# GRU, attention and AUGRU on one core: the last GRU step, the last softmax blocks and the way into the AUGRU rearranged

## The chip, the cores and the metric

The kernel runs on one core of one Trainium2 chip. Its engines work in parallel, each through its own queue in order: TensorE (PE, with its weight loads as PEld), VectorE (DVE), ScalarE (ACT), GpSimd (POOL) and SyncE (SP, which issues DMAs). The metric is the device time of one execution in microseconds (us).

## The reference

For 1024 samples and 100 steps of 128 features, the reference computes, all in float32:

```python
hist_sum = (hist * mask).sum(1) / length
keys = GRU(hist)                                  # all 100 states, 128 wide
score = relu-MLP([keys, q, keys - q, q * keys])   # 512 -> 80 -> 40 -> 1, q the item
attn = softmax(where(mask == 1, score, -inf), over the 100 steps)
pooled = einsum('bt,btd->bd', attn, keys)         # [1024, 128]
att_seq = pooled.T[:100]                          # row t weighs step t of the AUGRU
# AUGRU over keys, from a state of zeros
r = sigmoid(Wr [h, x]); u = att_seq[t] * sigmoid(Wu [h, x])
h = (1 - u) * h + u * tanh(Wh [h * r, x])
state = AUGRU state at step length - 1
scores = sigmoid-MLP([user, item, hist_sum, item * hist_sum, state])
```

The AUGRU therefore needs the attention over all 100 steps before its first step.

## The kernel before

The 1024 samples are two halves of 512; features lie on the partitions, samples along the free axis. `gru_phase` runs the 100 GRU steps, and `augru_phase` the 100 AUGRU steps after it. In both, the program order of each engine is written out by hand (`manual_schedule`), with the two halves staggered.

**GRU steps.** For each step `s` and half, `Half.gru` (L482 to L527) has PE compute the gates into PSUM banks, ACT the sigmoids and the tanh, and DVE the sums; the state `hn` is the key of that step. One step behind, `transpose` (L529 on) puts the key into blocks of 32 by 32 in a tile `kt` of four steps and stores `kt` to `keys_d` once it is full (L547, 1 MB for each half and four steps). `product` (L559) multiplies the key by the item, `attend` (L646) runs the three small layers of the score MLP packed in the PE, one layer for each of three successive steps, and `take` two calls later adds and applies the relu on DVE and ACT (L680 to L687) and stores a row of scores, by a small DMA, to `s_b` (L692). So the score of step `s` reaches `s_b` at loop step `s + 4`.

**Softmax by blocks.** When the last score of a block in `ENDS` is in, `softmax` queues three stages: `scores(0)` (transposes the scores of half 0), `tops` (those of half 1, the new maxima, the differences, L732 to L746) and `sums` (after `exponents`, the Exp on ACT, L752: products with the mask and the denominators, L755 to L769). `stage()` runs one a step on DVE, after half 0's GRU of the step. `sums` appends a rescaling (if it is not the first block) and the block's keys to each half's `todo`. `pool` (L572 to L583) takes one or two keys a step from it, on POOL, a product and a sum each. `history` (L476, L477) is also POOL's: the masked sum of the inputs, at the loop step of its input. Inputs `x` and masks are loaded two steps ahead by SP.

**After the last step.** From L850 on, what is left is written out: the last two attention layers, the softmax of the last blocks (whose `e` and products then use the PSUM banks named in `banks`), the first layer of the final MLP for what does not depend on the AUGRU (`features`, L613, stored at L623), and the last poolings, half 0's on POOL and half 1's on DVE. The pooled sums are masked (L908) and stored to `pooled_d` by eight DMAs on SP (L911).

**Into the AUGRU.** The AUGRU works on samples sorted by length, so that finished ones drop out. POOL gathers the sorted rows of `pooled_d` (`gather_weights`, L135), then sorted keys. PE transposes the keys of steps 0 and 1 (`load_key`, L987, L988), `first_step` (L935, L937) computes the gates of step 0, `open_gates` (L1001) the input parts of step 1. `sort_weights` (L952 to L967) spreads row 0 of the weights over the partitions by matmuls and forms the first state, transposes all 100 rows to `att_d`, and loads rows 1 and 2 from there, spread over the partitions (L974). `half_step` (L1020 on) is one step of one half: it closes the gates (L1005), weighs `pu` by the loaded row (L1036) and opens the next step. `sort_weights(0)` runs ahead of step 1, `sort_weights(1)` within half 0's step 1.

PSUM has eight banks: `ps` has six and `pa` two in the GRU, `ps3` seven and `pa3` one in the AUGRU, on the same memory in order. The AUGRU's first user of a bank waits for the last user of that bank in the GRU part.

## Time and profile before

| | us |
|---|---|
| median of 13 runs | 2091.33 (2087.88 to 2093.91) |
| the profiled execution, time | 2088.67 |
| the profiled execution, span of the trace | 2086.6 |
| GRU step, from one `r` (L502) to the next | 14.07 |
| last state of half 1 done | 1415.2 |
| last product with the mask (L908) done | 1452.8 |
| first gather of sorted weights | 1458.6 |
| first weights spread by PE (half 0) | 1465.2 |
| first candidate gate of step 1 closed by PE (L1005 on `r`) | 1482.9 |

Times inside the execution count from the start of the span. A line of the timeline gives start, duration, engine, line of the kernel, operation, output and inputs, shapes, and in brackets how long the engine had been idle and what ended that. A line by stretch gives for each engine the busy time and, in brackets, the number of instructions. A line of waits gives who waited for whom: total, times, longest.

### The profile page before, as it was taken

The page shows a single profiled execution, that of the slowest core. Times are in us where ns is not written, and L with a number is a line of the kernel's source. Part 1 is how long each engine was busy: PE and PEld are TensorE (multiplying, and loading weights), DVE is VectorE, ACT ScalarE, POOL GpSimd, SP SyncE. Part 2 cuts the span into 40 slices and gives each one's busy share as a digit, 9 for nine tenths or more (in the row PEclk, how much of TensorE's full clock was granted, in tenths as well). Part 3 has the DMA queues.
Part 4 walks back from the last instruction along what each step waited for, and adds up shares of the span by engine and source line. Part 5 has one row for each costly group of instructions (what it writes and reads, how often), then busy time and mean ns, then how long its engine had stood idle before and what let it go on. Part 6 is the DMA issues. An engine that isn't in the chain of part 4 may idle for free. (4 is left out here: it accounts for less than half of the span.)

```text
span 2086.6 us, 26766 instructions
## 1 busy us (share of the span) xinstructions
PE 2038.6 (98%) x8304; PEld 980.4 (47%) x8304; DVE 1748.8 (84%) x3040; ACT 827.6 (40%) x1511; POOL 1299.0 (62%) x1302
## 2 busy tenths in 40 slices
PE   8999999999999999999999999996799999999997
PEld 3343333333333333333333333333344556679897
DVE  6888999989989888989889888997467777888886
ACT  3334343433434333433343333343244444445454
POOL 0234939579796959595969587696645444444332
PEclk9999999999999999999999999998999999999999
DMA  4643233332234334333433222322533333333331
GB/s 119 114 93 101 88 102 110 95 96 89 88 104 111 112 100 121 110 97 108 132 102 98 86 82 84 102 93 69 154 92 116 94 93 96 99 97 101 84 73 34
DMA packets 254612, 205.60 MB, mean 99 GB/s; under 512 B 75847, under 2 KB 216875, under 8 KB 254459
## 3 DMA queue, kind: packets, MB, share of 16 engines
q1 hardware_dynamic: 242138, 171.36, 29.0%
q0 software_dynamic: 12320, 32.44, 5.5%
q8 instruction: 67, 1.10, 0.2%
q14 instruction: 87, 0.70, 0.1%
HBM read 147.68 MB, written 54.40 MB: 97 GB/s over the span
## 5 line engine op out<-in xcount | busy, mean ns | idle before, releaser
L490 PE MATMUL ps<-x,wih 128*128 128x512 f32 x1200 | 592.0, 603 | 4.0 <-DMA x<-in_hist_x 4.0
L490 PE MATMUL ps<-hn,whh 128*128 128x512 f32 x1188 | 574.6, 592 | 0.0
L490 PEld LDWEIGHTS ps<-x,wih 128*128 128x128 f32 x1200 | 220.9, 191 | 326.8 <-issue 254.0
L490 PEld LDWEIGHTS ps<-hn,whh 128*128 128x128 f32 x1188 | 225.9, 190 | 283.9 <-issue 275.5
L476 POOL TENSOR_TENSOR xm<-x,m 128x512 f32<-128x512 f32 x200 | 247.0, 1235 | 127.3 <-DMA m<-mask_d 127.0
L521 ACT ACTIVATE ps<-ps,bih 128x512 f32<-128x512 f32 x200 | 132.4, 662 | 469.8 <-DVE ps L520 469.8
L502 ACT ACTIVATE r<-ps,brz 128x512 f32<-128x512 f32 x200 | 137.4, 687 | 394.9 <-PE ps L490 393.8
L477 POOL TENSOR_TENSOR hist<-hist,xm 128x512 f32<-128x512 f32 x200 | 265.6, 1328 | 15.7
L583 POOL TENSOR_TENSOR pooled<-pooled,kw 128x512 f32<-128x512 f32 x190 | 253.4, 1334 | 14.9
L582 POOL TENSOR_TENSOR kw<-kt,e 128x512 f32<-128x512 f32 x190 | 217.1, 1143 | 64.1 <-DVE e L755 64.0
L159 POOL DMA_INDIRECT rows<-keys_d,idx_k x208 | 202.2, 972 | 84.7 <-POOL rows L158 53.3
L559 DVE TENSOR_TENSOR kq<-hn,item 128x512 f32<-128x512 f32 x200 | 227.3, 1176 | 0.0
L646 PE MATMUL pm<-hn,wk 128*32 128x512 f32 x1200 | 214.3, 600 | 6.0 <-DVE f L680 3.6
L646 PE MATMUL pm<-kq,wkq 128*32 128x512 f32 x1200 | 211.1, 594 | 0.0
L1013 ACT ACTIVATE c<-ph,bh 128x96 f32<-128x96 f32 (+42 forms) x198 | 96.7, 488 | 262.3 <-PE ph L1005 228.5
L646 PE MATMUL pm<-mv,w 128*32 128x512 f32 (+1 forms) x808 | 197.8, 603 | 1.1 <-ACT mv L685 0.9
L1029 DVE TENSOR_TENSOR pu<-pu,c 128x96 f32<-128x96 f32 (+42 forms) x197 | 88.8, 451 | 104.9 <-ACT c L1013 96.1
L680 DVE TENSOR_TENSOR f<-pm,q 128x512 f32<-128x512 f32 x200 | 128.5, 684 | 56.0 <-PE pm L646 56.0
L158 POOL COPY rows<-rest 128x1 f32<-128x1 f32 x208 | 39.0, 188 | 218.4 <-DVE rest L1039 213.2
L525 DVE TENSOR_TENSOR d<-hn,ps 128x512 f32<-128x512 f32 x198 | 136.1, 687 | 34.9 <-ACT ps L521 32.6
L526 DVE TENSOR_TENSOR d<-ps,d 128x512 f32<-128x512 f32 x200 | 138.4, 692 | 23.7 <-ACT ps L522 6.8
L520 DVE TENSOR_TENSOR ps<-ps,u 128x512 f32<-128x512 f32 x200 | 140.0, 700 | 21.6 <-PE ps L490 0.5
(171 smaller groups left out, 3014.1 us busy)
## 6 DMA issues: line engine op xcount, KB each, us to landing
x<-in_hist_x SPq DMA_DIRECT2D x212, 256.0 KB
keys_d<-kt SPq DMA_DIRECT2D x46, 1024.0 KB
m<-mask_d SPq DMA_DIRECT2D x200, 128.0 KB
keys_d<-kt SPq DMA_DIRECT2D x64, 64.0 KB
rows<-keys_d,idx_k POOLq DMA_INDIRECT x208
s_b<-mv SPq DMA_DIRECT2D x200, 8.0 KB
mask_i<-in_mask SPq DMA_DIRECT2D x8, 200.0 KB
at<-att_d SPq DMA_DIRECT2D x32, 48.0 KB
```

The costliest lines, as they stand in the source:

```text
L159: nc.gpsimd.indirect_dma_start(out=r[:, k, :], out_offset=None, in_=keys_d[q], in_offset=bass.IndirectOffsetOnAxis(ap=idx_k[:, k, i : i + ...
L476: nc.gpsimd.tensor_mul(d, x, m)
L477: nc.gpsimd.tensor_add(acc, acc, d)
L490: nc.tensor.matmul(p, lhsT=w[:, g, :], rhs=v, start=(j == 0), stop=(j == len(parts) - 1),)
L502: nc.scalar.activation(r, pr, AF.Sigmoid, bias=brz[:, 0:1])
L520: nc.vector.tensor_add(pi, pi, u)
L525: nc.vector.tensor_sub(d, h, pi)
L526: nc.vector.tensor_mul(d, pz, d)
L559: nc.vector.tensor_mul(kq, h, item[:, self.cols])
L582: eng.tensor_mul(d, k, w)
L583: eng.tensor_add(acc, acc, d)
L646: nc.tensor.matmul(p[i][s, :], lhsT=w[:, s], rhs=v, start=start, stop=stop)
```

## The change

Eight things change together.

- `ENDS` has blocks that end at 80, 86, 90, 93, 96, 98, 100 where it had 80, 88, 92, 96, 98, 100: one block more, and the block pending at the end of the loop (93 to 95) is of three steps and not of four.
- In step 99 no softmax stage runs. The block that becomes due there runs its first two stages after `attend(T - 1)`, and its Exp and third stage further down.
- From step 84 on, `history` takes the input of the following step (at 84 both), and in step 99 none; POOL also pools one key a half, or two, in step 99, after the products for the final MLP.
- In the written-out end the order of features, stages and poolings changes, the block pending there copies its weights later, and half 1 pools one key (not two) on DVE ahead of the next scores.
- The store of the last four keys moves from the transpose of the last step to after the last scores.
- The banks named in `banks` are assigned in another order.
- The pooled sums of half 1 come first and are stored by SP; those of half 0 are stored by ACT, from `augru_phase`, after the keys of step 0.
- The weights of step 1 are spread by matmuls and copied by ACT, as row 0 is spread by matmuls; only rows from 2 on go through `att_d`, and that store comes later, within step 1. The keys of step 1 go through the one bank of `pa3`.

```diff
-ENDS = (*range(8, 89, 8), 92, 96, 98, T)
+ENDS = (*range(8, 81, 8), 86, 90, 93, 96, 98, T)
...
-                x, m = self.x.pop(t), self.m.pop(t)
+                x, m = self.x[t], self.m.pop(t)
...
-                elif n == G - 1:
-                    row, part = divmod(q - WHOLE, 2)
-                    nc.sync.dma_start(
...
+                elif n == G - 1 and t < T - 1:
+                    self.store(q)
+
+            def store(self, q):
+                row, part = divmod(q - WHOLE, 2)
+                nc.sync.dma_start(
...
-        late, again = 6, 24
+        late, again, early_from = 6, 24, 84
...
-                    stage(2 if last else 1)
+                    stage(0 if last else 1)
...
-            for half in halves:
-                if s >= late:
-                    half.history(s)
-                else:
-                    half.x.pop(s)
+
+            for n_x in range(s + (s > early_from), min(s + (s >= early_from), T - 1) + 1):
+                for half in halves:
+                    if n_x >= late:
+                        half.history(n_x)
             for half in halves:
                 if last:
                     half.cross_features()
-                else:
-                    half.pool(2 if len(half.todo) > 7 or s >= 92 else 1, nc.gpsimd)
+            for half in halves:
+                half.pool(2 if len(half.todo) > 7 or s >= 92 else 1, nc.gpsimd)
...
-        banks.update(e=names[:2], kw=names[2], pt=names[3], f=names[4:])
+        banks.update(e=[b[0], b[1]], kw=b[3], pt=b[2], f=[b[4], b[5]])
...
         attend(T - 1)
-        stage()
-        e, _ = soft["e"]
-        copy = banks["e"][0][:, : NK * (G + 1)].rearrange("p (k n) -> p k n", n=G + 1)
-        nc.vector.tensor_copy(copy, e[:, :, : G + 1])
-        for half in halves:
-            half.todo = [((w[0], copy if w[0] is e else None), n, t) for w, n, t in half.todo]
-        halves[0].pool(T, nc.gpsimd)
+        stage(2)
+        weights = soft["e"][0]
+        exponents()
+        some(0, 1)
+        take(T - 1)
+        some(0, 1)
+        attend(T)
+        some(2)
         for half in halves:
             half.transpose(T - 1)
-        some(features[:1])
-        take(T - 1)
-        some(features[:1])
-        attend(T)
-        some(features[1:2])
-        halves[1].pool(2, nc.vector)
+        stage()
+        n = ENDS[-3] - ENDS[-4] + 1
+        copy = banks["e"][0][:, : NK * n].rearrange("p (k n) -> p k n", n=n)
+        nc.vector.tensor_copy(copy, weights[:, :, :n])
...
+        halves[0].pool(T, nc.gpsimd)
+        halves[1].pool(1, nc.vector)
         stage()
         take(T)
...
         attend(T + 1)
...
         stage()
         take(T + 1)
         exponents()
-        some(features[2:4])
+        some(3, 4)
+        some(5, 6)
+        for half in halves:
+            half.store((T - 1) // G)
         halves[1].pool(T, nc.vector)
-        some(features[4:6])
         stage()
         halves[0].pool(T, nc.gpsimd)
+        some(5, 6)
+        some(7)
         stage(2)
...
-        for half in halves:
+        for half in reversed(halves):
             t = blocked(s_bs[NH * (soft["j"] % 2) + half.i])
             nc.vector.tensor_mul(t, later["used"][:, half.ks, :], pooled[:, half.ks, :])
             to = pooled_d[half.cols, :].rearrange("(k r) (p c) -> p r k c", r=R, c=R)
-            for p in range(P // R):
-                nc.sync.dma_start(out=to[p], in_=t[p * R : (p + 1) * R])
+            later["att", half.i] = [(to[p], t[p * R : (p + 1) * R]) for p in range(P // R)]
+        for to, t in later["att", 1]:
+            nc.sync.dma_start(out=to, in_=t)
...
-        def sort_weights(i, r, gates):
+        def weight_row(t, i, p):
             for g in range(GH):
                 nc.tensor.matmul(
+                    p[:, ts(g, P)],
+                    lhsT=sorted_rows[i][:, g, t : t + 1].to_broadcast([P, P]),
                     rhs=ident,
...
+        def first_state(i, p):
+            weight_row(0, i, p)
+            u, h = gates[i]
+            nc.vector.tensor_mul(p, p, u)
+            nc.vector.tensor_mul(h3[i], p, h)
+
+        def first_weights(i, p):
+            weight_row(1, i, p)
+            at = att[1, i] = wp.tile([P, HB], F32, name="at", bufs=6)
+            nc.scalar.copy(at, p)
+
+        def store_weights(i, p):
             for g in range(GH):
-                nc.tensor.transpose(p[:, ts(g, P)], r[:, g, :], ident)
+                nc.tensor.transpose(p[:, ts(g, P)], sorted_rows[i][:, g, :], ident)
             rows_t = wp.tile([P, HB], F32, name="att_t", bufs=2)
             nc.vector.tensor_copy(rows_t, p)
             nc.sync.dma_start(out=att_d[i], in_=rows_t[:T, :])
-            for t in (1, 2):
-                load_att(t, i)
+            load_att(2, i)
...
-                p = bank("pk3") if t < 2 else pa.tile([P, HB], F32, tag="a", name="pk3")
+                p = pa.tile([P, HB], F32, tag="a", name="pk3")
...
             if t == 1 and i == 0:
-                sort_weights(1, sorted_rows[1], gates[1])
+                store_weights(0, pa.tile([P, HB], F32, tag="a", name="pw"))
+                first_state(1, spare)
+            elif t == 1:
+                first_weights(1, spare)
             nc.vector.tensor_mul(pu, pu, att.pop((t, i))[:, :w])
...
+            if t == 1 and i:
+                store_weights(1, spare)
             if t + 2 < T:
                 load_att(t + 2, i)
...
-        sorted_rows = [gather_weights(i) for i in range(NH)]
         for i in range(NH):
             load_key(0, i)
+        for to, t in later["att", 0]:
+            nc.scalar.dma_start(out=to, in_=t)
+        sorted_rows = [gather_weights(i) for i in range(NH)]
         gates = [first_step(i) for i in range(NH)]
...
-        sort_weights(0, sorted_rows[0], gates[0])
+        spare = bank("spare")
+        first_state(0, pa.tile([P, HB], F32, tag="a", name="first"))
+        first_weights(0, spare)
```

More of the change, by code (lines that the diff above doesn't have):

```diff
@@ L544, in transpose @@
                         )
-                elif n == G - 1:
-                    row, part = divmod(q - WHOLE, 2)
-                    nc.sync.dma_start(
-                        out=keys_d[WHOLE + row].rearrange("(k p) m -> p k m", p=P)[
-                            :, self.ks, ts(part, G * R)
-                        ],
-                        in_=kt.rearrange("p k n c -> p k (n c)"),
-                    )
+                elif n == G - 1 and t < T - 1:
[3 more added lines that the diff above has]
+                nc.sync.dma_start(
+                    out=keys_d[WHOLE + row].rearrange("(k p) m -> p k m", p=P)[
+                        :, self.ks, ts(part, G * R)
+                    ],
+                    in_=self.kt[q].rearrange("p k n c -> p k (n c)"),
+                )
             def product(self, t):
@@ L853, in gru_phase, with some @@
         all_of(rest)
-        names = [ps.tile([P, HB], F32, tag="g", name="last") for _ in range(6)]
-        banks.update(e=names[:2], kw=names[2], pt=names[3], f=names[4:])
+        b = [ps.tile([P, HB], F32, tag="g", name="last") for _ in range(6)]
+        banks.update(e=[b[0], b[1]], kw=b[3], pt=b[2], f=[b[4], b[5]])
         features = [half.features(g) for half in halves for g in range(GH)]
-        def some(these):
+        def some(*these):
             for f in these:
-                next(f)
+                next(features[f])
         take(T - 2)
@@ L867, in gru_phase @@
         attend(T - 1)
-        stage()
-        e, _ = soft["e"]
-        copy = banks["e"][0][:, : NK * (G + 1)].rearrange("p (k n) -> p k n", n=G + 1)
-        nc.vector.tensor_copy(copy, e[:, :, : G + 1])
-        for half in halves:
-            half.todo = [((w[0], copy if w[0] is e else None), n, t) for w, n, t in half.todo]
-        halves[0].pool(T, nc.gpsimd)
+        stage(2)
[6 more added lines that the diff above has]
+        some(2)
         for half in halves:
             half.transpose(T - 1)
-        some(features[:1])
-        take(T - 1)
-        some(features[:1])
-        attend(T)
-        some(features[1:2])
-        halves[1].pool(2, nc.vector)
+        stage()
[3 more added lines that the diff above has]
+        for half in halves:
+            half.todo = [
+                ((w[0], copy if w[0] is weights else None), n, t) for w, n, t in half.todo
+            ]
+        halves[0].pool(T, nc.gpsimd)
+        halves[1].pool(1, nc.vector)
         stage()
         take(T)
-        some(features[1:2])
+        some(2)
         attend(T + 1)
-        some(features[2:4])
+        some(3, 4)
         stage()
@@ L890, in gru_phase @@
         exponents()
-        some(features[2:4])
+        some(3, 4)
+        some(5, 6)
+        for half in halves:
+            half.store((T - 1) // G)
         halves[1].pool(T, nc.vector)
-        some(features[4:6])
         stage()
         halves[0].pool(T, nc.gpsimd)
+        some(5, 6)
+        some(7)
         stage(2)
-        some(features[4:6])
         exponents()
-        some(features[6:])
-        some(features[6:])
+        some(7)
         stage()
@@ L945, in gather_weights @@
             return r
-        def sort_weights(i, r, gates):
-            first = pa.tile([P, HB], F32, tag="a", name="first")
+        def weight_row(t, i, p):
             for g in range(GH):
                 nc.tensor.matmul(
-                    first[:, ts(g, P)],
-                    lhsT=r[:, g, 0:1].to_broadcast([P, P]),
+                    p[:, ts(g, P)],
+                    lhsT=sorted_rows[i][:, g, t : t + 1].to_broadcast([P, P]),
                     rhs=ident,
@@ L958, in sort_weights @@
                 )
-            u, h = gates
-            nc.vector.tensor_mul(first, first, u)
-            nc.vector.tensor_mul(h3[i], first, h)
-            p = pa.tile([P, HB], F32, tag="a", name="pw") if i else bank("pw")
+        def first_state(i, p):
[8 more added lines that the diff above has]
+        def store_weights(i, p):
             for g in range(GH):
-                nc.tensor.transpose(p[:, ts(g, P)], r[:, g, :], ident)
+                nc.tensor.transpose(p[:, ts(g, P)], sorted_rows[i][:, g, :], ident)
             rows_t = wp.tile([P, HB], F32, name="att_t", bufs=2)
```

## The prediction

> **What bounds the kernel now.** I read the page's forty slices first, then the busy time by stretch, then the waits of DVE and PE between 1399 and 1490 us, and last the timelines of that stretch, because the change touches nothing else.
>
> The slices: PE is at nine tenths everywhere but for a dip at slices 28 to 29, and POOL and DVE dip there too.
>
> ```profile
> PE   8999999999999999999999999996799999999997
> DVE  6888999989989888989889888997467777888886
> ```
>
> By stretch (PE, its weight loads, DVE, ACT, POOL; then TensorE clock, DMA share, GB/s): the reader is to see a PE that is full before and after, and holes between.
>
> ```profile
> 1300.00:1400.00 100.00, 100.00 (x397) 38.66 (x396) 91.62 (x136) 41.12 (x64) 77.98 (x64) 1.00 0.33 102
> ...
> 1432.60:1452.80 20.20, 8.23 (x47) 7.64 (x46) 18.66 (x46) 3.40 (x10) 11.32 (x10) 0.81 0.12 43
> 1452.80:1458.60 5.80, 5.80 (x18) 3.02 (x17) 0.00 (x0) 4.02 (x6) 0.00 (x0) 0.77 0.53 90
> ...
> 1470.60:1482.90 12.30, 2.27 (x12) 1.70 (x11) 3.06 (x5) 0.10 (x1) 6.05 (x7) 0.72 0.70 216
> 1482.90:1488.50 5.60, 5.60 (x11) 2.35 (x11) 2.31 (x5) 2.60 (x4) 3.75 (x8) 0.70 0.51 174
> 1500.00:1900.00 400.00, 399.90 (x1318) 241.85 (x1317) 309.71 (x604) 178.92 (x327) 185.44 (x316) 1.00 0.36 100
> ```
>
> So GRU steps and AUGRU steps are PE-bound, and the passage between them (about 1406 to 1486 us) is a chain of waits. Time taken from that chain moves all later work forward one for one; time on DVE or POOL inside the steps is free while PE stays full. The waits in the passage:
>
> ```profile
> DVE first L960 <- PE first L952: 13.6, 1, 13.6
> DVE first L960 <- remote: 7.8, 1, 7.8
> DVE last L732 <- DMA s_b<-mv: 4.1, 1, 4.1
> ...
> PE pk L987 <- DVE pooled L583: 9.7, 1, 9.7
> PE pw L964 <- DVE h L961: 9.1, 1, 9.1
> PE pm L646 <- DVE f L680: 3.6, 1, 3.6
> ```
>
> Four links can be read: a DVE that is late in the last step (PE waits 3.6), scores that land late (4.1), a PE that waits for the end of pooling before it starts the AUGRU (9.7), and the start of the AUGRU itself (13.6, 7.8, 9.1). In DVE's timeline the cause of the 3.6 and the end of pooling stand as
>
> ```profile
> 1406.63 0.72 DVE L732 STREAM_TRANSPOSE pt<-s_b 128x512 f32<-128x512 f32 x1
> ...
> 1409.38 1.38 DVE L746 TENSOR_TENSOR e<-e,top 128x128 f32<-128x128 f32 x1
> 1410.67 0.74 DVE L510 SCALAR_TENSOR_TENSOR u<-ps,bhh,r 128x512 f32<-128x512 f32 x1
> ...
> 1451.48 1.28 DVE L908 TENSOR_TENSOR s_b<-used,pooled 128x512 f32<-128x512 uint8 x2
> ```
>
> **The change part by part.** I follow milestones in the profiled execution.
>
> *Stages out of step 99.* DVE's eight softmax instructions from 1406.63 to 1410.67 leave. Half 1's gate inputs were ready at 1405.65, so its state is done 4.04 us sooner: 1415.2 becomes 1411.2. They are not saved but moved: DVE does them after the products of the last step. PE, which finished the attention of step 98 at 1412.2, finds the bank free at about 1411.9 instead of 1415.9, so its 3.6 us hole closes, and with it most of the half clock behind it (clock 0.59 from 1415.2 to 1422.8). What then limits is the product kq (2.7 us, to 1415.7); attention of step 99 ends near 1417.4, not 1422.8.
>
> *Shorter last blocks.* One block more: per block about 7.8 us of DVE in three steps (0.95, 3.2 and 3.6 by the rows of steps 95 to 97), and two more rescalings on POOL (1.07 each). They fall in steps with a PE of 100.00 in 100; three-step blocks take DVE 39 to 41 us of 42.2, so six such steps in a row (93 to 98) still fit: cost 0. If that cover is gone the excess of DVE, at most a microsecond or two, is paid. The block pending at the end has 3 keys instead of 4: one product and one sum less for each half in the tail, 1.4 us on DVE, 2.3 on POOL.
>
> *History a step ahead.* Four POOL instructions per step (4.9 us) run one step sooner; no DMA moves, since x and mask are loaded two steps ahead. In step 99 POOL drops 4.9 us of history and takes two poolings of 2.4 us. By POOL's work per step it is clear near 1414 instead of 1421.5. Worth nothing itself, but the small DVE instructions at 1418.9 to 1422.5 (L755 1.35, L759 1.03, L760 0.97) cost 0.2 each where POOL is idle: 0 to 2.5 us, I take 1.5.
>
> *Last keys late.* The two stores of 1 MB held the DMA from 1423.5 to 1434, and scores issued at 1425.8 landed at 1432.7, nearly 7 us. The other small stores land about 2 us after issue. Issued after the last scores, the stores let the scores of step 97 land near 1424.5, ahead of DVE: the 4.1 us go. The stores then run from about 1430 to 1440, with the feature store of half 1 queued behind them on SP (read only much later) and the pooled stores 6 us behind; if that margin is gone, up to 4 us come back.
>
> Tail sum, from hn of half 1 to the end of pooling. DVE is the path: 4.1 (scores) + 1.4 (pooling) + 1.5 (contention), and the 4.0 put back as about 3.2 since fewer keys are in it; with the 4.0 of step 99 that is 4.0 + 4.1 + 1.4 + 1.5 − 3.2 = 7.8 at best. Laying the instructions end to end, with the ACT table load (1.28) now behind the tops, I get 5.3 with every contended duration kept and 6.5 with none. I take 6: the last product ends at 1446.8 instead of 1452.8.
>
> *Pooled stores on two queues, banks reordered.* SP issued eight stores from 1452.19 to 1456.31, and the first gather began 2.3 after that, at 1458.63. Four on SP and four on ACT take 2.2 after the last product: 4.5 instead of 5.9, a gain of 1.4. No ACT DMA stands in this trace; I price it as SP's 0.5 each. Against it speaks the Trainium skill, "DMA: Bandwidth & Descriptors", section "Issuing engines are not separate DMA queues": both run on the same 16 engines and only issue time is saved. The row has share 0.53 with one queue, so two cannot double the rate: by the rule alone 0 to 1, by the issue row 1.4. I take 1. The keys of step 0 now use a bank free long before, so the 9.7 us wait goes, but step 0's gates still need a bank read by the last pooling, and ACT has the four issues (2 us), a table load, four activations (2.4) and key copies in a single bank ahead of the opening of step 1. That path has PE ready at about 1460, the gathered weights are there by 1458.4 (first gather 1451.8, and 6.6 to the first row's matmul as from 1458.63 to 1465.24). First weights: 1465.2 becomes 1460, 5.3 sooner. Loss of cover: the old kernel had both paths at 1465; here PE and ACT are later than the gathers, and a slow ACT queue would show directly.
>
> *Weights of step 1 by matmuls.* Removed from the path: store, two loads of 256 KB, and the wait for them; added: four matmuls of 128 columns for each half (1.05 a row, as at 1465.24) and an ACT copy (0.58). From the first weights to the candidate gate of step 1: two rows 2.1, DVE's lag 0.4, two gates 1.7, transposes 0.6, half 1's row 1.05, key of step 2 with its wait 1.1: 7.0, where the old trace has 17.6 (1465.24 to 1482.86). In the 17.6 lie 7.8 us (1470.6 to 1478.4) that no recorded instruction explains: DVE waits for half 1's first row, whose matmuls are recorded as over at 1470.8, while DMA is at share 0.70. Bounds: nothing of it recurs, or all 7.8. The order stays (eight gathers of weights, then eight of keys), but 512 KB of broadcast loads are gone from the burst, so I take the first. The weights of step 2 still go through memory (store issued at 1468.56, loads at 1471.04, some 4 us more by DMA's busy stretch): about 7 us after DVE's copy, and half 0 needs them 11 us on, half 1 about 9: hidden, with 2 us to spare.
>
> Sum: 5.3 + 10.6 = 15.9. A full clock in step 1 (now 0.70 over 5.6 us) would add 1.7; I give that back for the pauses that remain. So 16 off: 2088.67 becomes 2072.7 in the profiled execution, which lies 2.66 below the median of the runs; from the median, 2075.3, said as **2076**.
>
> **Rivals.** *The unexplained wait recurs.* For: its cause is unseen and the key gathers follow as before. Against: less DMA, and half 1's row comes later after its gather. It would give 2076 + 7.8, about 2083.
>
> *Only the tail gains, or the start alone.* Late key stores meet the pooled stores, or ACT with its queue of issues becomes the bound and hands back the tail's 6 and more: 4 us gained, about 2087; at worst no measurable change. For it: ACT's key copies, which open step 1, sit behind four issues that wait for the last product. Against: 6 us between the key stores and the pooled stores, and issues of 0.5 on SP.
>
> *Slower: the clock stays down.* PE idles from about 1436 to 1445, so step 0 starts at half clock. In the trace such spells end soon: 0.72 over 12.3 us and 0.70 over 5.6 us make about 10 us at half, and it is whole from 1500. The skill's "TensorE: Matmul & The Clock Gate", section "Seeing it yourself", warns that the gate has been seen stuck for over 50 us. By the row the cost is within the 1.7 above; by the rule, each us at half costs half a us of a full PE, so from 40 us on (16 + 4) it decides: 60 us give 2090 to 2106. No run here shows it.
>
> **How the numbers follow.** Forecast case 0.50 (2071 to 2080: tail 5.3 to 7.8, opening 1458 to 1463). The wait recurs 0.30 (2079 to 2087). Partial gain 0.10, of which a third within 0.2%, and slower 0.06 by the clock, some 0.04 for a gain beyond 2071. About 0.2%, 4.2 us, is what a measurement of this kernel can tell from no change. Leaving out two in ten, the range is 2070 to 2086. Faster: 0.50 + 0.30 + 0.04 + 0.06 = 0.90; same 0.04; slower 0.06.
>
> **What would show it.** Right: no softmax instruction between the two halves' states of step 99, no 3.6 us wait of PE; no wait of DVE for the scores; pooling over near 1447; first weights near 1460 and the candidate gate of step 1 near 1467; a flat 100% of PE before 1406 and after 1490. Wrong: a DVE wait of several us at half 1's first state, an ACT that opens step 1 after 1463, PE gaps in steps 93 to 98, or weights of step 2 awaited.

## The result, and the profile after

The changed kernel takes 2082.86 us (median of 10 runs, 2081.53 to 2085.87), the kernel before on the same chip 2090.39 us (46 runs, 2087.53 to 2093.91). The ratio is 0.9966, with a 95% interval of 0.9958 to 0.9974: 7.5 us faster. The forecast was 15.3 us. The direction and the range held, but half of the gain is missing. The profiled execution of the changed kernel took 2083.95 us (span 2082.2), against 2088.67 (span 2086.6) before. These two single executions lie only 4.7 us apart. The profiled run of before was 1.7 us under its median and that of after 1.1 us over its own, so the traces are read for places and the medians for the size.

The milestones that the prediction followed, in us from the start of the span. "Half 1's gate" is the second candidate gate of step 1. The prediction did not follow it, and it turns out to be the one that counts.

| | before | forecast | after |
|---|---|---|---|
| last state of half 1 | 1415.2 | 1411.2 | 1415.0 |
| last product done | 1452.8 | 1446.8 | 1449.2 |
| first gather of weights | 1458.6 | 1451.8 | 1454.5 |
| first weights on PE | 1465.2 | 1460 | 1461.5 |
| first candidate gate of step 1 (half 0) | 1482.9 | 1467 | 1472.9 |
| half 1's gate of step 1 | 1490.1 | (1474) | 1486.6 |
| end of the span | 2086.6 | 2070.6 | 2082.2 |

The number in brackets carries the old 7.2 us between the two gates on, as the sum did without saying so. Stage by stage, before to after: last state 0.2 earlier; from there to the last product 37.6 to 34.2; to the first gather 5.8 to 5.3; to the first weights 6.6 to 7.0; to half 1's gate 24.9 to 25.1. That makes 3.5 us at half 1's gate. Half 0's gate comes 10.0 us earlier, and 6.5 of these are lost again before half 1's.

Slices of the changed kernel's page, PE and DVE. PE's dip reads 7 and 8 where it read 6 and 7, and DVE is at nine tenths instead of eight in slices 24 and 25, ahead of it:

```profile
PE   8999999999999999999999999997899999999997
DVE  6888999998989888989888899997467777888886
```

By stretch, with the columns as before (PE, weight loads, DVE, ACT, POOL; then TensorE clock, DMA share, GB/s). The tail's DVE is busy 15.4 of 16.6 us. Step 1 still has a hole: PE works 9.97 of the 13.7 us before half 1's gate, at a clock of 0.65. From that gate on PE is full at full clock:

```profile
1432.60:1449.20 16.60, 6.67 (x34) 5.66 (x35) 15.37 (x37) 2.59 (x8) 11.33 (x10) 0.77 0.57 176
1449.20:1454.50 5.30, 4.79 (x11) 2.00 (x10) 0.02 (x1) 2.91 (x4) 0.05 (x1) 0.75 0.62 101
1461.50:1472.90 11.40, 6.14 (x38) 4.66 (x37) 2.77 (x4) 1.91 (x3) 8.66 (x10) 0.97 0.51 138
1472.90:1486.60 13.70, 9.97 (x29) 4.85 (x29) 6.17 (x10) 3.08 (x5) 6.11 (x12) 0.65 0.44 136
1486.60:1500.00 13.40, 13.40 (x40) 6.40 (x39) 7.49 (x12) 6.74 (x11) 8.19 (x15) 1.00 0.66 200
```

The waits of the same passage, 1399 to 1490 us. The 4.1 us for the scores are gone, and PE's wait for DVE's `f` fell from 3.6 to 1.7. A wait "remote" ends when the awaited semaphore is raised at a moment at which the profile shows no instruction ending. In place of the one such wait of 7.8 us there are two on DVE, 5.0 and 3.5:

```profile
DVE first L973 <- PE pu L1020: 13.4, 1, 13.4
ACT k L1007 <- remote: 8.6, 1, 8.6
PE pu L947 <- DVE pooled L587: 7.0, 1, 7.0
DVE spare L973 <- remote: 5.0, 1, 5.0
DVE att_t L986 <- remote: 3.5, 1, 3.5
PE pm L650 <- DVE f L684: 1.7, 1, 1.7
```

The first of the two in the timeline: the transposes into `pw` are recorded as over at 1466.5, and the copy that waits for nothing else starts at 1471.36. By then GpSimd has been issuing gathers since 1454 with pauses of 0.30 us only:

```profile
1465.93 0.60 PE L984 MATMUL pw<-ident,att_r 128*128 128x128 f32 x4
...
1470.82 0.95 POOL L135 DMA_INDIRECT rows<-keys_d,idx  x1 [0.30 <-issue]
1471.36 0.69 DVE L986 COPY att_t<-pw 128x512 f32<-128x512 f32 x1 [3.52 <-remote]
```

### The profile page after: what moved, and what is told of

It is laid out like the page before. It is cut to its first block, busy times and chain, and to the rows that moved or that the text cites. A ratio compares the mean times of both kernels' runs of the same rounds, so it can differ in the third digit from the quotient of the medians.

```text
span 2082.2 us, 26811 instructions
## 1 busy us (share of the span) xinstructions
PE 2038.5 (98%) x8320; PEld 981.8 (47%) x8320; DVE 1758.1 (84%) x3050; ACT 830.8 (40%) x1516; POOL 1304.2 (63%) x1306
## 5 line engine op out<-in xcount | busy, mean ns | idle before, releaser
L526 DVE TENSOR_TENSOR d<-ps,d 128x512 f32<-128x512 f32 x200 | 138.4, 692 | 23.4 <-ACT ps L522 6.2
```

The source lines that it names most:

```text
L526: nc.vector.tensor_mul(d, pz, d)
```

## The experiments

The runs of one group were made on one chip, beside the kernel before. The chips differ: the kernel before takes 2089.76 us on chip A, 2073.75 on B, 2097.85 on C, 2098.04 on D and 2074.22 on E. That difference became part of the answer. "To half 1's gate" is the time from the first weights on PE to half 1's candidate gate of step 1, from each trace.

| run | chip | median, us | ratio to before (95%) | last state | first weights | to half 1's gate |
|---|---|---|---|---|---|---|
| before (first trace) | – | 2090.39 | 1 | 1415.2 | 1465.2 | 24.9 |
| after (first trace) | – | 2082.86 | 0.9966 (0.9958–0.9974) | 1415.0 | 1461.5 | 25.1 |
| e1 key gathers spread | A | 2081.01 | 0.9948 (0.9933–0.9963) | 1414.5 | 1461.0 | 15.4 |
| e2 the same, in before | A | 2087.02 | 0.9978 (0.9968–0.9989) | 1415.4 | 1465.2 | 18.4 |
| e3 old block ends | A | 2081.97 | 0.9953 (0.9938–0.9969) | 1410.6 | 1459.4 | 25.0 |
| e4 history in its own step | A | 2084.91 | 0.9968 (0.9955–0.9982) | 1414.0 | 1462.5 | 23.3 |
| e5 four gathers first | B | 2067.57 | 0.9968 (0.9956–0.9980) | 1415.0 | 1461.4 | 15.2 |
| e7 e5 and old block ends | B | 2068.87 | 0.9976 (0.9967–0.9986) | 1411.8 | 1460.9 | 15.2 |
| e8 last keys stored early | B | 2067.92 | 0.9969 (0.9957–0.9981) | 1416.4 | 1462.8 | 13.7 |
| e9 burst with a quarter of the bytes | B | 2066.80 | 0.9965 (0.9953–0.9977) | 1414.5 | 1461.0 | 13.7 |
| f1 before, unedited | C | 2097.22 | 0.9998 (0.9989–1.0007) | 1415.5 | 1466.1 | 26.9 |
| f2 after, unedited | C | 2090.49 | 0.9964 (0.9950–0.9977) | 1416.8 | 1463.2 | 25.4 |
| f3 old order of PSUM banks | C | 2088.90 | 0.9963 (0.9951–0.9975) | 1414.7 | 1461.2 | 23.4 |
| f4 weights of step 1 by DRAM | C | 2088.54 | 0.9955 (0.9942–0.9969) | 1415.3 | 1461.7 | 25.4 |
| h1 four gathers first | D | 2086.26 | 0.9943 (0.9930–0.9956) | 1414.9 | 1461.3 | 21.4 |
| h2 burst with a quarter of the bytes | D | 2089.01 | 0.9957 (0.9943–0.9970) | 1415.3 | 1461.8 | 23.4 |
| h3 four first, rest spread | D | 2085.11 | 0.9937 (0.9924–0.9951) | 1414.6 | 1461.1 | 16.8 |
| h4 after, unedited | D | 2087.53 | 0.9953 (0.9939–0.9966) | 1414.4 | 1460.9 | 23.3 |
| i1 four first, two per half step | E | 2068.43 | 0.9972 (0.9962–0.9982) | 1414.5 | 1461.0 | 14.7 |
| i2 i1 and old block ends | E | 2069.02 | 0.9975 (0.9965–0.9985) | 1412.9 | 1461.8 | 14.5 |

Two theories stood at the outset. The first: the extra softmax block, which the prediction took as free, fills DVE and delays the loop. The second: the burst of eight gathers of key rows delays completions of PE in step 1.

### Where the loop lost its 4 us

The edit of e3 puts the old ends back:

```diff
-ENDS = (*range(8, 81, 8), 86, 90, 93, 96, 98, T)
+ENDS = (*range(8, 89, 8), 92, 96, 98, T)
```

> The kernel after, with the block ends of before (88, 92, 96, 98, 100): one block fewer in the loop, a pending block of four keys. Theory (the extra block fills DVE in steps 90 to 98 and delays the last state): PE no longer slips in steps 93 to 98 (2.5 us), the last state of half 1 is done near 1411 instead of 1415, DVE and POOL each have one key more in the tail (1.4 and 2.3 us): 1 to 3 us faster than after. Rival (history a step ahead fills DVE by contention with POOL): the slip stays, last state near 1415, and the time is 1 to 2 us slower than after.

With the old ends the last state comes at 1410.6, which is the forecast's 1411.2. With the new ends it comes at 1415.0, although the stages have left step 99 there too. The busy time by stretch of one step shows what changes. The changed kernel first:

```profile
1272.00:1286.00 14.00, 14.00 (x57) 5.40 (x56) 13.16 (x19) 4.99 (x9) 10.18 (x9) 1.00 0.19 57
...
1356.00:1370.00 14.00, 12.77 (x49) 4.95 (x51) 13.12 (x20) 5.49 (x9) 13.61 (x12) 1.00 0.44 134
```

and the same stretches with the old block ends:

```profile
1272.00:1286.00 14.00, 14.00 (x58) 5.34 (x57) 11.80 (x17) 4.95 (x8) 11.27 (x9) 1.00 0.20 57
...
1356.00:1370.00 14.00, 14.00 (x57) 5.34 (x57) 13.02 (x20) 6.29 (x10) 13.53 (x12) 1.00 0.53 156
```

DVE (third engine) is at 13.1 to 13.3 of 14 in all ten stretches from 1272 to 1412 of the changed kernel. With the old ends it rests in four of the first six (11.8 to 12.8). In the ten stretches together it is busy 131.4 us, with the old ends 128.2: 3.2 us more. That DVE has no slack left to catch up fits this, and PE, which is full with the old ends there, is short by 1.2 us in the stretch from 1356. Which wait carries the delay from step to step was not traced. Attention of step 98 starts 2.5 us later than in the kernel before (1410.27 against 1407.75), and the last state is 4.4 us later than with the old ends. A DVE as full as this does no harm in single steps: the kernel before has four such stretches from 1356 on, 13.05 to 13.30 us, with a full PE. The first of them:

```profile
1356.00:1370.00 14.00, 14.00 (x57) 5.36 (x56) 13.05 (x20) 5.60 (x9) 13.61 (x12) 1.00 0.46 142
```

The tail gives part of it back. From the last state to the last product it takes 34.2 us with the new ends and 36.5 with the old, because the pending block has one key less. Net, e3 is 2.1 us ahead at the first weights and its ratio is 0.9953 against 0.9966, with overlapping intervals. On chips B and E the old ends gain nothing on top of moved gathers (e7 beside e5, i2 beside i1 below). The block's extra end costs 4.4 us in the loop in this pair of traces (3.9 beside e1, which ran on e3's chip), 3.3 on chip B and 1.6 on E, and returns 2.3 to 2.4 in the tail; what is left is between nothing and 2 us.

History taken in its own step again, e4:

```diff
-            for n_x in range(s + (s > early_from), min(s + (s >= early_from), T - 1) + 1):
+            for n_x in (s,):
```

> The kernel after, with the history of each input at its own step again and also in step 99. Theory (extra block): the slip of PE in steps 93 to 98 stays (2 us or more), POOL has 4.9 us more in step 99 and is the later one in the tail: 0 to 4 us slower than after. Rival (history ahead makes the slip): no slip, last state near 1411, the time 2 to 4 us faster than after if POOL does not bound the tail.

The slip stays (last state 1414.0), so history on POOL isn't its cause. From there to the last product it takes 36.3 us where the changed kernel takes 34.2, so the last product is 1.1 us later; the ratio, 0.9968, can't be told from 0.9966.

### What delays PE's completions in step 1

The edit of e1, on the changed kernel, and of e2, on the kernel before:

```diff
-        all_of(gathers(1))
+        early_rows = gathers(1)
...
                 half_step(t, i)
+                for _ in range(2 if t < 3 else 0):
+                    next(early_rows, None)
```

> The kernel after, with the eight gathers of the keys of steps 4 to 7 no longer in one burst behind the gathers of the weights, but two after each half step of steps 1 and 2. Theory (the burst of 2 MB holds up PE's completions): the two unexplained waits of DVE at the transposed rows and at half 1's first state, 3.5 and 5.0 us, shrink to under 1 us each, and the time falls by 6 to 8.5 us, to about 2075 to 2077. Rival (the weights' own gathers, or the TensorE clock, hold it): both waits stay and the time is within 2 us of 2083.

> The kernel before, with the same spreading of the eight key gathers. Theory (burst): DVE's 7.8 us wait at half 1's first weights shrinks to under 1 us and the time falls by 5 to 8 us, to about 2083 to 2085. Rival (weights' gathers or clock): the wait stays, time within 2 us of 2090.4.

Both waits of DVE for a remote increment vanish in e1, and half 1's gate comes 15.4 us after the first weights instead of 25.1. In the kernel before, the 7.8 us wait falls to 2.5. The medians gain less than either run's theory said: e2 is 2.7 us under before, and e1's ratio is 0.9948 beside the changed kernel's 0.9966, with overlapping intervals. In e1 the gain is handed back between 1490 and 1518, by a wait of the same kind and not by late keys. PE transposes keys of step 4 without having waited for a DMA, the transposes are recorded as over at 1500.66, and ACT's copy of them starts 6 us later:

```profile
1500.06 0.60 PE L1006 MATMUL pk<-ident,rows 128*128 128x128 f32 x4
...
1506.69 0.58 ACT L1007 COPY k<-pk 128x502 f32<-128x502 f32 x1 [6.36 <-remote]
```

Then the same gathers in another order, half of them ahead of the weights while GpSimd is idle (e5), and with the old block ends as well (e7):

```diff
+        key_rows = gathers(1)
+        for _ in range(GH):
+            next(key_rows)
         sorted_rows = [gather_weights(i) for i in range(NH)]
...
-        all_of(gathers(1))
+        all_of(key_rows)
```

> The changed kernel, but the first half's four gathers of key rows of steps 4 to 7 (128 KB... 256 KB each, 1 MB of the 2 MB) are issued ahead of the eight weight gathers, while GpSimd stands idle from 1447.7 to 1454.4; the second half's four stay after the weights. Theory A (the burst of eight key gathers delays the PE's completions by 3.5 and 5.0 us in step 1, 8.5 in all): only four gathers are left behind the weights, so at least half of the 8.5 us goes, and since no gather is issued late the gain is not handed back at steps 4 to 8 as when they were spread: 4 to 8 us below the changed kernel, 2075 to 2079. Theory B (the waits have nothing to do with these gathers): both waits stay as they are and the time is that of the changed kernel, 2082 to 2084. Theory C (the key transfers get in front of the weights' gathers, which come from the pooled weights in DRAM): first weights at 1463 to 1465 instead of 1461.5 and the time is 2083 to 2086.

> As the run with four key gathers issued first, and the softmax blocks end where they ended before the change (88, 92, 96, 98). Theory (the extra block's work slips the loop by 2.5 to 4 us; the burst's delay is another, independent matter): the two add up to 2 us and 4 to 8 us, so 2073 to 2078, 1 to 2 us below the run with the four gathers alone. Rival (both gains meet the same limit, the recurrence's start in step 1 or later waits for keys): no better than the better of the two alone, 2079 to 2082.

And the burst kept in place and count, with a quarter of its bytes (e9, which leaves out the keys of steps 4 to 7):

```diff
-                gather(r[:, g, :], keys_d[q], g, i)
+                if q:
+                    gather(r[:, g, :P], pooled_d, g, i)
+                else:
+                    gather(r[:, g, :], keys_d[q], g, i)
...
-                    nc.tensor.transpose(p[:, ts(g, P)], r[:, g, ts(n, P)], ident)
+                    nc.tensor.transpose(p[:, ts(g, P)], r[:, g, ts(0 if q else n, P)], ident)
```

> The changed kernel with the burst of eight gathers kept at its place and in its count, but each reads one 512-byte row per partition from the pooled weights instead of a 2048-byte key row: 0.5 MB instead of 2 MB (the real keys of steps 4 to 7 are left out, and one block is used for all four steps). If the bytes on the DMA queues delay the PE's completions, the two waits of step 1 (3.5 and 5.0 us) shrink to a quarter or vanish, and the time is 4 to 8 us below the changed kernel, 2075 to 2079. If the eight GpSimd issues (about 1.25 us each) do it, the waits stay at 7 to 9 us together and the time is 2081 to 2084.

These three say nothing on the burst, because this chip shows no such wait whatever the kernel. The fourth run on it, e8, has the burst unedited. Its eight key gathers are

```profile
L135 POOL DMA_INDIRECT rows<-keys_d,idx x8: 952/957/957, 1466.0 to 1474.8; - x8
```

and the same two DVE instructions that waited 3.5 and 5.0 us wait 1.0 and 0.2:

```profile
DVE att_t L984 <- PE spare L982: 1.0, 1, 1.0
DVE spare L971 <- PE spare L960: 0.2, 1, 0.2
```

So the wait depends on the chip. The next group asked whether it also depends on the kernel, by running both kernels unedited.

> The kernel before, unedited, for its trace on the chip that the next three runs are made on. The run with the last keys stored early kept the burst of eight key gathers and showed no wait for a remote increment in step 1, on a chip where the kernel before took 2073.75 us. Theory D (the wait belongs to the chip's state and to no kernel; the kernel before has it wherever the changed kernel has it): on a chip with about 2074 us for this kernel the 7.8 us wait of the first att row is gone (under 1 us), on one with about 2090 us it is 7 to 9 us. Theory E (the wait comes from this kernel's own order of instructions): 7 to 9 us on any chip, and the difference between chips lies elsewhere.

> The changed kernel, unedited. Theory D: 0.9960 to 0.9972 of the kernel before, as on the first chip; the two waits of 3.5 and 5.0 us are gone together with that of the kernel before, or there together with it, so that the gain is made of the tail (about 3.4 us from the last state to the last product), the gathers (0.6 and 0.4 us) and step 1 (2.5 to 3 us), 6 to 7.5 us in all. Theory E: without its waits the changed kernel gains the full 15 us of the forecast, 0.992 to 0.994.

On chip C the kernel before shows its wait again, of the same length:

```profile
DVE first L960 <- remote: 7.8, 1, 7.8
```

The changed kernel has one of 5.7 us on DVE (`att_t`), and the ratio is 0.9964. So the wait, where it appears, appears in both kernels, as theory D has it. On chips B and E no trace of the kernel before was taken, but its time there is 15 us and more below that on A, C and D. The version nearest to the changed kernel there, e8, is 5.8 us below it, against 7.4 on chip C and 10.5 on D (h4, below), with intervals that overlap: no difference of the gain with and without the wait is seen. A change that had removed a wait of 7.8 us would be expected to gain less where there is none to remove.

The last step was to repeat the two edits on a chip with the wait, beside the unedited kernel (h4), with a third that leaves no burst (h3: as e5, but the remaining four one in each half step):

```diff
                 half_step(t, i)
+                next(key_rows, None)
```

> The changed kernel with the first half's four key gathers ahead of the weights' gathers, as in the earlier run of this edit, beside the unedited changed kernel on the same chip. Burst theory (where the unedited kernel shows waits for remote increments of 6 to 9 us in step 1): with four gathers left behind the weights the waits fall to 4 us or less, and second half's gate of step 1 comes 15 to 19 us after the first weights instead of 25; time 4 to 8 us below the unedited one. Rival (not the burst): 23 to 26 us and the time of the unedited one within 1 us. Where the unedited kernel shows no such wait, both give the same time within 1 us.

> The burst of eight gathers in its place, each of 512-byte rows of the pooled weights instead of 2048-byte key rows (the real keys of steps 4 to 7 are left out). If the bytes delay the PE's completions and the unedited kernel shows the waits: waits 2 us or less, second half's gate 14 to 17 us after the first weights, time 5 to 9 us below the unedited one. If the eight issues on GpSimd do it: waits and time as in the unedited one, within 2 us.

> The first half's four key gathers ahead of the weights and the second half's four one in each half step from step 1 on, so that no burst is left. Burst theory: no wait for a remote increment on any chip, second half's gate 14 to 16 us after the first weights, and with one gather in a half step nothing is handed back at step 4; on a chip with the waits 6 to 10 us below the unedited changed kernel. Rival (spread gathers come late for step 4 as when two went in each half step): 1 to 3 us below it.

> The changed kernel, unedited, for its trace on the chip of these runs. If the waits for remote increments belong to the chip: present (6 to 9 us in step 1) on a chip where the kernel before takes about 2090 us or more, absent where it takes about 2074 us; ratio to the kernel before 0.9960 to 0.9972 on either.

The unedited kernel from 1465 to 1475 us, the stretch of the burst; the last two columns are DMA share and GB/s:

```profile
1465.00:1475.00 10.00, 3.26 (x19) 2.65 (x18) 1.38 (x2) 1.91 (x3) 6.69 (x7) 0.77 0.70 190
```

and its waits there:

```profile
PE pk L1006 <- DVE att_t L986: 6.7, 1, 6.7
DVE att_t L986 <- remote: 4.3, 1, 4.3
```

With a quarter of the bytes (line numbers 3 higher):

```profile
1465.00:1475.00 10.00, 3.06 (x16) 1.85 (x14) 1.00 (x2) 1.91 (x3) 7.53 (x8) 0.82 0.21 54
```

```profile
PE pk L1009 <- DVE att_t L989: 6.7, 1, 6.7
DVE att_t L989 <- remote: 4.3, 1, 4.3
```

The DMA share falls from 0.70 to 0.21, the wait stays at 4.3 us to the tenth, and the time is 1.5 us above the unedited kernel's, with overlapping intervals. The bytes aren't it. With four of the eight issues moved ahead (h1) the wait is 2.9 us, and half 1's gate comes at 21.4 us instead of 23.3, between the burst theory's 15 to 19 and the rival's 23 to 26. With no burst after the weights there is no wait on DVE for a remote increment; PE is busy 8.13 of the same 10 us at full clock, and the gate comes at 16.8:

```profile
1465.00:1475.00 10.00, 8.13 (x36) 4.91 (x37) 6.09 (x10) 4.42 (x8) 3.48 (x6) 1.00 0.30 78
```

The times fall far less than the burst theory said: h1 is 1.3 us and h3 2.4 us below the unedited kernel, with overlapping intervals. In h3 half 1's gate is 6.3 us ahead, and 2.1 us are lost again where step 4 is opened, by a late completion too. The copy that waits there is of half 0's keys of step 4, whose gathers were issued by 1453.5; their transposes are recorded as over at 1494.82, and ACT copies them at 1498.64.

The semaphore records in the traces, which none of the views above lists, tell which side is late. Between 100 and 2060 us, each trace of the first pair and of chips A, C and D has 26 to 41 increments by PE that stand more than 0.15 us behind the end of the last matmul that can have made them, up to 10 us behind. Some then come in a bunch: in h4 five within 0.2 us, from 1476.48 to 1476.67. On chips B and E a trace has at most one, 0.19 us behind. The increments of DVE, ACT and GpSimd follow their instructions by 0.01 us on every chip. So PE's signal is late, and not the engine that waits for it.

These late increments stand in the later part of long rows of gathers (pauses under 0.85 us): from 1465 on in the changed kernel's row of 16, which starts at 1454; in e1 again from 1488 to 1509.5, where the spread gathers and the paced ones of later steps make one row of 26; in h3 from 1498.6 to 1501.5, at the end of a row of 19. So spreading the burst took one long row away and made another. Length isn't all: the rows of 10 and 9 that begin with the weights' gathers in e1 and h3 end with some late increments, and so do some rows of 7 to 9 after 1870, while rows of 6 to 13 that start between 1475 and 1800 have none. That a long row brings them on fits this, and isn't shown.

What goes with the wait is the row of back-to-back issues on GpSimd (0.95 us each and 0.30 between), not what they move. What passes between those issues and a completion of PE, and why two chips of five are free of it even in rows of 39 (e8), no run here shows; it stays open. The traces with late increments also lack 6 to 10% of the increment records of PE, DVE, ACT and GpSimd, and those of B and E lack none; whether the two belong together isn't shown either.

The last pair tried to avoid both the burst and h3's loss at step 4, which their expectations put down to late keys (two gathers in each half step, all gone by 1479 us instead of 1491), i2 with the old block ends too:

```diff
                 half_step(t, i)
+                for _ in range(2):
+                    next(key_rows, None)
```

> The changed kernel with the first half's four key gathers ahead of the weights' gathers and the second half's four two by two in the half steps of step 1, so that none is left for step 2. If a burst of eight issues is what delays the PE's completions, four in two pairs delay them little: second half's gate of step 1 at 15 to 19 us after the first weights; and since the last key gather leaves GpSimd before 1483 instead of 1491, step 4 waits for no keys and the gates of step 5 come 2 us earlier against that of step 1 than with one gather in a half step: ratio to the kernel before 0.992 to 0.9935 on a chip where that takes about 2090 us or more. Rival (step 4's late keys were not from those gathers, but from the paced ones of step 8 that share GpSimd): no better than 0.9937.

> The same gathers as in the run beside it, four ahead and two by two, with the softmax blocks ending at 88, 92, 96 and 98 as before the change. Theory (without the extra block the loop ends 3 to 4 us earlier and the tail gives back 2 to 3 of them): within 1.5 us of the run beside it, rather below than above. Rival (the loop's 4 us come through to the end): 3 to 4 us below it.

They fell on chip E, where no wait for a remote increment appears, so they don't tell what the order is worth elsewhere. The gates of the step that lost time in h3 take 11.1 us in both, against 13.2 there, but so they do in every run on chips B and E. The old ends come 1.6 us earlier out of the loop and 0.8 later to the first weights: nothing gained.

### Single parts undone

Three parts of the change were put back alone. The store of the last keys, e8:

```diff
-                elif n == G - 1 and t < T - 1:
+                elif n == G - 1:
...
-        for half in halves:
-            half.store((T - 1) // G)
```

> The changed kernel with the store of the last steps' keys put back in the transpose, ahead of the scores' transfers on SyncE's queue. Theory of the prediction (a late store takes away the 4.1 us in which the last scores waited for their transfer): the wait of the transposed scores comes back, last product 3 to 4 us later than 1449.2, time 2085 to 2087. Rival (the wait has been hidden by the reordered tail anyhow, the store's place is worth nothing): 2082 to 2084.

The scores don't wait, and the tail is as long as in the changed kernel (34.2 us). SyncE's queue in e8 shows the 2 MB of keys standing after the transfer that DVE waited for, since the transposes that feed the store now come after `attend(T)`:

```profile
1417.70 8.29 SPq L696 DMA_DIRECT2D s_b<-mv  x4
1426.09 2.25 SPq L551 DMA_DIRECT2D keys_d<-kt  x2
1428.43 6.05 SPq L696 DMA_DIRECT2D s_b<-mv  x4
```

In the kernel before, the two key stores were issued at 1423.46 and the awaited scores at 1425.78, behind them. So the reordered tail takes the 4.1 us away without the late store, which adds nothing to it. The order of the PSUM banks, f3:

```diff
-        banks.update(e=[b[0], b[1]], kw=b[3], pt=b[2], f=[b[4], b[5]])
+        banks.update(e=[b[0], b[1]], kw=b[2], pt=b[3], f=[b[4], b[5]])
```

> The changed kernel with the two PSUM banks of the tail exchanged back (the pooling's product bank and the transposes' bank as before the change). Theory (the new order lets the tail's pooling or transposes start before the features are read): last product 1 to 2 us later after the last state than the 34.2 us of the changed kernel, time 0.5 to 2 us above it. Rival (the order is worth nothing, since the banks come free before they are asked for): within 0.5 us of the changed kernel.

The tail is 34.2 us long and the ratio 0.9963, as in the unedited kernel on that chip (34.2 and 0.9964). And the weights of step 1 through memory, f4:

```diff
-            load_att(2, i)
+            for t in (1, 2):
+                load_att(t, i)
...
-                store_weights(0, pa.tile([P, HB], F32, tag="a", name="pw"))
-                first_state(1, spare)
-            elif t == 1:
-                first_weights(1, spare)
+                first_state(1, pa.tile([P, HB], F32, tag="a", name="first"))
+                store_weights(1, spare)
...
-            if t == 1 and i:
-                store_weights(1, spare)
...
-        first_weights(0, spare)
+        store_weights(0, spare)
```

> The changed kernel, but the weights of step 1 are read back from DRAM as before the change (rows transposed, stored, and row 1 and row 2 loaded with a broadcast), for both halves. Theory of the prediction (the store and load are a round trip of some 4 to 5 us on the way to the first candidate gate; the matmul and the copy take 2): first candidate gate 2.5 to 4 us later after the first weights, time 2.5 to 4 us above the changed kernel. Rival (step 1 is bound by something else, such as the key transposes and the single PSUM buffer): within 1 us of the changed kernel.

Half 0's gate comes 17.5 us after the first weights, 2.9 us later than in the unedited kernel on that chip (14.5): the forecast's round trip is there. But half 1's gate comes at 25.4 us in both, and the time is no longer. On a chip with the wait, the matmuls in place of the round trip are worth nothing in the end. On one without it this wasn't run.

## Why the prediction was right or wrong

**Stages out of step 99: right, then undone.** With the block ends of before, the last state is at 1410.6 (forecast 1411.2, before 1415.2). With those of the change it is at 1415.0.

**"Shorter last blocks ... cost 0": the first step that failed.** The sum 39 to 41 of 42.2 us was read as room. Four stretches with DVE at 13.05 to 13.30 of 14 us, as in the kernel before, leave PE full; ten in a row left nothing to absorb a stage. It cost 4.4 us here, and 1.6 to 3.9 in the three pairs on one chip; the fallback price in the prediction, "at most a microsecond or two", was too low in all but one. The gain in the tail, put at 1.4, measured 2.3.

**The tail: right in sum, partly for a wrong reason.** From last state to last product 37.6 us became 34.2, where the forecast had 35.6. The scores' wait went as forecast, but through the order of transposes and attention and not through the late store. Of the 3.4 us, 2.3 go with the shorter pending block. With history back in its own step the tail is 2.1 us longer too, so the parts don't simply add up, and they were not taken apart further. In the time, history ahead and the bank order can't be told from nothing.

**Two queues for the pooled stores: a small gain.** Last product to first gather: 5.8 to 5.3 us (5.9 to 5.2 on chip C). The prediction weighed the issue row (1.4) against the Trainium skill's "DMA: Bandwidth & Descriptors", section "Issuing engines are not separate DMA queues" (0 to 1), and took 1. The rule was nearer. ACT issues cost what SP's do (median 0.52 and 0.49 us). PE was the later of the two paths to the first weights, as forecast: in h1 the weights' gathers start 1.8 us later than in h4 on the same chip (1455.7 and 1453.9) and the first weights only 0.4 later (1461.3 and 1460.9).

**First weights to the first candidate gate, 17.6 to 7.0: the step that failed, and the largest.** Measured, 17.6 became 11.4 at half 0's gate, and 24.9 became 25.1 at half 1's, so of the 10.6 us nothing is left there. The 7.0 us are about right for this kernel on a chip without the wait (6.3 in e8). Three things are wrong in the step. It took 7.8 us of old waiting as removed by the change, and the change touches nothing of what goes with them: the burst of issues on GpSimd stands where it stood, and waits of 5.0 and 3.5 us took their place. The step ended at half 0's gate, and the sum let this shift everything after it; half 1's gate is the one that PE's full stretch starts from, and it came only 3.5 us earlier. And the remaining 2.8 us, for matmuls in place of the round trip, are there at half 0's gate in f4 and gone at half 1's. The argument "512 KB of broadcast loads are gone from the burst" weighed bytes, and bytes don't matter here. The prediction had named its own sign of being wrong, a DVE wait of several us at half 1's first state, and that is the wait of 5.0 us.

**The rivals.** "The unexplained wait recurs" named the mechanism and its 2083 us are the measured 2082.9. Part of that is chance: at half 1's gate its sum, 16 less 7.8, is 8.2 us, where the traces show 3.5 and 4.3 (chips of the first pair and C). The loop's lost 4 us are missing in it, and the medians differ by 3 us more than the first pair of profiled executions does. On the chips with the wait PE's increments come late again near the end of the run, and in some executions of either kernel ACT then waits for them (up to 3.9 us: once in f1 and f4, twice in h1, all between 1900 and 2000). That is of the size of the 3 us; that it makes them isn't shown. The rival in which the clock stays down fell: 0.65 over 13.7 us, and 1.00 from half 1's gate on, 1486.6. The skill's "TensorE: Matmul & The Clock Gate", section "Seeing it yourself", warns of a gate stuck for over 50 us; no run here shows that.

**Where the gain is.** The traces show 3.5 to 4.3 us of it at half 1's gate: stages moved and order of the tail, less the slip of the loop. The fastest version here, beside the changed kernel on chip D, is h3 with 2085.11 against 2087.53 us, ratios to before 0.9937 (0.9924 to 0.9951) and 0.9953 (0.9939 to 0.9966). It beats the kernel before clearly; that it beats the changed one is likely but not settled, since the intervals overlap.

## What to carry to other kernels

A wait whose cause can't be named isn't to be counted as a gain: ask whether the change removes what stands beside it in time, here the row of gather issues, and if it doesn't, carry the wait over. Judge slack on an engine by how full it is over many steps in a row, not by whether each step's sum fits. When a burst is spread, look where its parts go: here they made another row, and a part of the wait came back there. And follow a shift to the last instruction that the next full stretch of PE waits for; a milestone of one half says nothing if the other half ends later.

## What the runs showed of the hardware that was not expected

- Sixteen indirect gathers issued by GpSimd back to back (1.25 us each with the pause) go with waits of DVE of 3.5 to 9.8 us (the longest in f4) for completions of PE whose matmuls are recorded as over, in the first pair and on three chips (A, C, D). PE's semaphore increments alone are late there, up to 10 us; those of DVE, ACT and GpSimd come 0.01 us after their instructions. In h4 and h2 the wait is the same, 4.3 us, with the key gathers' bytes cut to a quarter (DMA share 0.70 and 0.21). On chips B and E there is no such wait with the same issues.
- One and the same kernel differs by 1.2% between chips (2073.75 to 2098.04 us), and the two fast chips are those without the wait. Of the 15.8 us between the spans of e8 and of the changed kernel's first trace, 10.1 are there at half 1's gate (1476.5 and 1486.6), though e8 comes to the first weights 1.3 us later; the rest, 5.7 us, arises after that. The changed kernel's trace has late increments by PE between 1933 and 2044 too, and e8's none.
- With DVE recorded at 13.1 to 13.3 us of 14 in ten stretches in a row, the last state came 4.4 us later than with four of the first six at 11.8 to 12.8. Four such stretches in the kernel before cost PE nothing (14.00 of 14 us).
